# Layer 0's bias: channels sorted by sign, sums of two groups of keys folded into one last product

## The chip, the cores and the metric

The kernel runs on one core of a Trainium2 chip. The core has a matrix engine (TensorE, PE in the profile), a vector engine (VectorE, DVE), an activation engine (ScalarE, ACT), a general engine (GpSimd, POOL), and SyncE (SP), which here only issues DMAs. They share an on-chip memory of 128 partitions (SBUF) and the matrix engine's output memory (PSUM). The metric is the device time of one execution in microseconds (us); the median of several runs counts.

## What is computed

The program is four layers on an image tensor of shape (2, 512, 32, 32). Layer 0 is an attention whose keys are sampled at learned places, followed by an MLP; layers 1 to 3 are other attentions and aren't touched. Layer 0 has 2 x 8 heads, 1024 queries and 64 keys per head. Each pair of query and key gets a bias from a small network with 128 hidden channels:

```python
pos = grid_q[:, :, None, :] - grid_kv[:, None, :, :]
bias = jnp.sign(pos) * jnp.log1p(jnp.abs(pos))
bias = jax.nn.relu(bias @ cpb_w1 + cpb_b1)
bias = jax.nn.relu(bias @ cpb_w2 + cpb_b2)
bias = (bias @ cpb_w3 + cpb_b3).reshape(b, GROUPS, H * W, Hd * Wd)
sim = jnp.einsum('bhid,bhjd->bhij', qh, kh) + bias
attn = jax.nn.softmax(sim, axis=-1)
```

The second product, 128 x 128 channels for 16 x 1024 x 64 pairs, is the bulk of the layer's work. The change concerns what happens between it and the third product, `@ cpb_w3`, which sums 128 channels, each with its weight, to one number.

## The kernel before

**The weights.** `last_weights` and `fold_weights` (L252 to L280) prepare the third product. The magnitude of each `cpb_w3` is multiplied into the columns of `cpb_w2` and into the bias, which a Relu lets through, so that only its sign is left. The 128 hidden channels are cut into four blocks q of 32 channels; row r of each block has its own sign. `flip` holds the sign of blocks 0 to 2 relative to block 3, `ends` that of block 3.

**The quads.** The work goes in quads of four keys, 256 in all: for each head u (16), each o (8) and each jj (2). A quad (u, o, jj) makes these steps:

- `first_hidden` (L633): DVE writes the first hidden layer of the four keys, four tiles of 128 channels x 1024 queries, one custom add with Relu each, for the quad that comes next. The two parts of the sum come from `table`, which loads the positions (L572, a DMA on SyncE with two buffers) and scales them on GpSimd (L574) and DVE (L618).
- `second_hidden` (L664): for each block q, eight products of 128 rows and 32 columns give a PSUM tile whose 128 partitions are four keys x 32 channels. ScalarE applies Relu with bias (L669) into a tile `h2q` of SBUF; there are 2, 3, 2 and 5 buffers for the four q.
- The four blocks are added into one tile with their signs: block 0 is flipped on ScalarE (L671), block 1 on GpSimd where jj is 1 (L673) and on ScalarE where it is 0 (L675), block 2 on GpSimd (L680). Block 0 goes into 1 by an accumulating DMA that GpSimd issues (L656), block 2 into 3 by an add on GpSimd (L682), and block 1 into 3 by another accumulating DMA, `join`, which is issued in the next quad after its own q = 1.
- `last_product` (L696): for each (u, o), four products of 128 rows and 32 columns (two jj, two halves of the queries) go to four column tiles of the array. The stationary operand is a window of `ends` with four columns that aren't zero, one for each key of the quad; over the eight o they fill 32 rows of the scores of the head.

```python
z = self.second_hidden(u, o, jj, h1, i + 1 == len(quads))
if jj == 1:
    held.append((u, o, (first, z)))
else:
    first = z
    if len(held) == 2:
        v, last, zs = held.pop(0)
        self.last_product(v, last, zs, sims, ps_s)
```

**The order.** In layer 0 the order of the instructions on PE, ACT, DVE and POOL is the order in which the program writes them down; each engine works through its own list and waits where an operand or a buffer isn't ready. SyncE's list is ordered by the framework's scheduler. Steps for the next pair of heads (`offsets`, `sampled`) and for the head that was finished (`attend`, `projection`) are put between the quads, one per quad. After the last quad come the last products of o = 6 and 7, the softmax of the last head and the output projection (`share`, L236; `project_one`, L795), in which DVE makes the final adds (L654, L682) itself.

**The start.** Until the first quad, about 21 us, `offsets` runs for the first pair of heads, with a convolution as products by diagonal matrices (L422, L425), and matmuls of ones (L152) fill TensorE. L597 spreads the first positions over all partitions; L561 turns x, and L480 makes the second q.

Of the kernel before, what the change touches and what calls it, by code (L numbers as in the profile page):

```python
# [34 lines left out]
    ("cpb_w1", 2), ("cpb_b1", 1), ("b2r", 4), ("w3r", 4), ("cpb_b3", 1),  # L35
# [11 lines left out]
NGRID = G_MID + 1  # L47

# [6 lines left out]
class Net:  # L55
# [40 lines left out]
    def layer0(self):  # L96
# [3 lines left out]
        with ExitStack() as ctx:  # L100
# [15 lines left out]
            self.weights = self.last_weights(keep)  # L116
# [22 lines left out]
            nc.vector.tensor_copy(self.taps, self.colr("dw_w", len(TAPS)))  # L139
            self.jj = 1  # L140
# [3 lines left out]
            with self.tc.manual_schedule(engines=engines):  # L144
# [9 lines left out]
                warm(11)  # L154
                for n, _ in enumerate(self.offsets(pairs[0], 0, ps)):
                    if n == 1:
                        warm(5)
                    elif n == 2:
                        first_tr = self.turn(pairs[0], 0, ps)
                        for t in (1, 2):  # L160
                            self.normed(pairs[t], t, nc.gpsimd)
                    elif n == 4:
                        warm(11)
# [5 lines left out]
                quads = [(u, o, jj) for u in range(2 * BP) for o in range(8) for jj in range(2)]  # L169
# [10 lines left out]
                held, self.join = [], None  # L180
                for i, (u, o, jj) in enumerate(quads):
                    self.jj = jj
                    if o == 1 and jj == 1 and u % 2 == 0 and u // 2 + 1 < BP:
# [7 lines left out]
                    z = self.second_hidden(u, o, jj, h1, i + 1 == len(quads))  # L191
                    if jj == 1:
                        held.append((u, o, (first, z)))
                    else:
                        first = z
# [18 lines left out]
                self.last_product(*held[0], sims, ps_s)  # L214
# [4 lines left out]
                self.last_product(*held[1], sims, ps_s)  # L219
# [29 lines left out]
    def last_weights(self, keep):  # L249
# [4 lines left out]
        nc = self.nc  # L254
        self.w3row = keep.tile([P, P], F32, tag="row", name="w3row")
        nc.scalar.dma_start(self.w3row, self.io["cpb_w3"].partition_broadcast(P))
        yield
        w3 = self.colr("w3r", 4)
        self.magb = keep.tile([P, 4], F32, tag="magb", name="magb")
        nc.vector.scalar_tensor_tensor(self.magb, w3, -1.0, w3, ALU.mult, ALU.max)  # L260
        nc.vector.tensor_tensor(self.magb, self.magb, self.colr("b2r", 4), ALU.mult)
        sign = keep.tile([P, 4], F32, tag="sign", name="sign")
        nc.vector.tensor_scalar(sign, w3, 0.0, 2.0, ALU.is_ge, ALU.mult)
        nc.vector.tensor_scalar(sign, sign, -1.0, None, ALU.add)
        self.flip = keep.tile([P, 3], F32, tag="flip", name="flip")
        nc.vector.tensor_tensor(self.flip, sign[:, 0:3], sign[:, 3:4].to_broadcast([P, 3]), ALU.mult)
        yield
        self.ends = keep.tile([P, 60], F32, tag="ends", name="ends")
        nc.gpsimd.memset(self.ends, 0.0)
        for k in range(4):  # L270
            rows = slice(32 * k, 32 * k + 32)
            nc.gpsimd.tensor_copy(self.ends[rows, 28 + k : 29 + k], sign[rows, 3:4])
        yield
        nc.vector.tensor_copy(self.ys, self.grid[:, G_Y : G_Y + NB])
        yield

    def fold_weights(self):
        nc, row = self.nc, self.w3row
        nc.vector.scalar_tensor_tensor(row, row, -1.0, row, ALU.mult, ALU.max)
        nc.vector.tensor_tensor(self.l0w2, self.l0w2, row, ALU.mult)  # L280
# [9 lines left out]
    def odd(self):  # L290

        while self.jj == 0:
            yield

    def advance(self, behind, enough):

        self.jj = 1
# [1664 lines left out]
```

## Time and profile before

| What | us |
|---|---|
| Median of 3 runs (lowest 3308.89, highest 3309.51) | 3309.51 |
| The profiled execution | 3310.24 |
| Its span, from first to last instruction | 3308.4 |
| First and last record of L664 (layer 0's second product) | 21.4 and 1975 |
| PE busy with L664 / L696 | 1790.1 / 133.3 |
| DVE busy with L633 | 1180.8 |
| ACT busy with L669 / L671 / L675 | 1121.7 / 291.3 / 145.6 |
| POOL busy with L682 / L656 / L680 / L673 | 610.5 / 451.6 / 446.5 / 143.6 |

The granted clock of TensorE was 1.00 throughout. In the lines of the profile, "L664" is line 664 of the kernel; "h<-hp,magb" says what is written from what, by tile names without numbers; "128x1024" is partitions x elements, "128*32" the size of the stationary operand; x16384 counts instructions. A product in fp32 shows as two records. A releaser behind "<-" is what ended the idle time before the instruction. "PEld" is the weight load. Records of TensorE overlap, so their mean duration isn't what one costs; the chain (the work that ended last, in order of time) and windows serve for that.

### The profile page before, as it was taken

The page shows a single profiled execution, that of the slowest core. Times are in us where ns is not written, and L with a number is a line of the kernel's source. Part 1 is how long each engine was busy: PE and PEld are TensorE (multiplying, and loading weights), DVE is VectorE, ACT ScalarE, POOL GpSimd, SP SyncE. Part 2 cuts the span into 40 slices and gives each one's busy share as a digit, 9 for nine tenths or more (in the row PEclk, how much of TensorE's full clock was granted, in tenths as well). Part 3 has the DMA queues.
Part 4 walks back from the last instruction along what each step waited for, and adds up shares of the span by engine and source line. Part 5 has one row for each costly group of instructions (what it writes and reads, how often), then busy time and mean ns, then how long its engine had stood idle before and what let it go on. Part 6 is the DMA issues. An engine that isn't in the chain of part 4 may idle for free.

```text
span 3308.4 us, 59878 instructions
## 1 busy us (share of the span) xinstructions
PE 3293.4 (100%) x24966; PEld 1223.5 (37%) x24966; DVE 2367.5 (72%) x2735; ACT 2038.2 (62%) x2139; POOL 2190.8 (66%) x1682
## 2 busy tenths in 40 slices
PE   9999999999999999999999999999999999999999
PEld 4332333332333333333333334444465533455333
DVE  7877777877776677777777665564565689855897
ACT  7887887888887588887887771111121366222662
POOL 6887887887877687887887874333223458634575
PEclk9999999999999999999999999999999999999999
DMA  7787887787787687887788762111000100000001
GB/s 181 160 163 152 161 165 154 160 164 154 162 158 142 119 162 150 162 162 155 159 159 180 160 133 112 39 51 38 0 1 0 39 1 1 14 1 13 1 1 52
DMA packets 102671, 342.64 MB, mean 104 GB/s; under 512 B 12656, under 2 KB 14832, under 8 KB 99312
## 3 DMA queue, kind: packets, MB, share of 16 engines
q0 software_dynamic: 73296, 266.90, 41.3%
q1 hardware_dynamic: 28080, 69.75, 7.5%
q8 instruction: 201, 3.29, 0.4%
q10 hardware_dynamic: 1008, 2.00, 0.2%
q14 instruction: 86, 0.70, 0.1%
HBM read 67.27 MB, written 4.46 MB: 22 GB/s over the span
## 4 chain that ended last, share of the span: by engine, by line
PE 91%; DVE 5%; POOL 2%; issue 1%; DMA 1%; ACT 0%; DVEq 0%; POOLq 0%; ACTq 0%
PE hp L664 50%; PE s L1512 5%; PE o L1541 5%; PE sim L696 3%; PE qk30P L1287 1%; PE qk20P L1287 1%; PE m_2P L842 1%; PE m_7P L842 1%; PE m_6P L842 1%; PE m_4P L842 1%; PE m_1P L842 1%; PE qk31P L1287 1%; PE qk21P L1287 1%; PE m_5P L842 1%; PE m_0P L842 1%; PE m_3P L842 1%
## 5 line engine op out<-in xcount | busy, mean ns | idle before, releaser
L664 PE MATMUL hp<-h,w 128*32 128x512 f32 x16384 | 1790.1, 592 | 1.0 <-ACT h L669 1.0
L633 DVE CUSTOM_DVE_ANT_1 h<-tx,bank 128x1024 f32<-128x1024 f32 (+1 forms) x1028 | 1180.8, 1210 | 362.2 <-PE hp L664 290.9
L669 ACT ACTIVATE h<-hp,magb 128x1024 f32<-128x1024 f32 x1024 | 1121.7, 1111 | 352.7 <-PE hp L664 342.0
L664 PEld LDWEIGHTS hp<-h,w 128*32 128x32 f32 x16384 | 528.1, 110 | 1212.0 <-issue 1158.0
L656 POOL DMA_DIRECT2D h<-h x509 | 451.6, 1021 | 356.3 <-ACT h L675 293.5
L682 POOL TENSOR_TENSOR h<-h,h 128x1024 f32<-128x1024 f32 x255 | 610.5, 2394 | 21.3
L680 POOL TENSOR_SCALAR h<-h,flip 128x1024 f32<-128x1024 f32 x256 | 446.5, 1744 | 1.0 <-ACT h L669 0.9
L1516 ACT ACTIVATE e<-s 128x1024 f32<-128x1024 f32 x256 | 262.0, 1025 | 181.2 <-PE s L1512 174.1
L671 ACT ACTIVATE h<-h,flip 128x1024 f32<-128x1024 f32 x256 | 291.3, 1138 | 0.0
L1541 PE MATMUL o<-e,v 64*64 64x512 f32 x2048 | 265.2, 589 | 2.5 <-DVE q L1580 2.5
L1512 PE MATMUL s<-q,k 64*64 64x512 f32 x2048 | 265.9, 591 | 0.0
L1523 POOL TENSOR_TENSOR some<-some,e 128x1024 f32<-128x1024 f32 x64 | 167.8, 2622 | 26.5 <-ACT e L1516 23.8
L1521 POOL TENSOR_TENSOR some<-e,e 128x1024 f32<-128x1024 f32 x32 | 76.1, 2378 | 141.7 <-DVE sum L1530 102.7
L673 POOL TENSOR_SCALAR h<-h,flip 128x1024 f32<-128x1024 f32 x128 | 143.6, 1122 | 30.2 <-ACT h L669 28.9
L675 ACT ACTIVATE h<-h,flip 128x1024 f32<-128x1024 f32 x128 | 145.6, 1138 | 0.0
L1528 DVE TENSOR_TENSOR sum<-sum,e 128x1024 f32<-128x1024 f32 x64 | 124.2, 1940 | 29.6 <-ACT e L1516 27.0
L696 PE MATMUL sim<-h,ends 128*32 128x512 f32 x1024 | 133.3, 592 | 0.0
L1541 PEld LDWEIGHTS o<-e,v 64*64 64x64 f32 x2048 | 77.9, 133 | 145.3 <-issue 134.9
L812 POOL TENSOR_TENSOR mlp_w<-mlp_w 128x512 f32<-128x512 f32 x16 | 21.8, 1360 | 159.5 <-DMA mlp_w<-in_mlp_w 121.4
L1512 PEld LDWEIGHTS s<-q,k 64*64 64x64 f32 x2048 | 76.5, 133 | 133.2 <-issue 117.2
L903 ACT ACTIVATE mh<-mh,cols 128x512 f32<-128x512 f32 x64 | 46.1, 721 | 124.3 <-DVE mh L921 65.4
L1526 DVE TENSOR_TENSOR sum<-e,e 128x1024 f32<-128x1024 f32 x32 | 81.1, 2534 | 31.7 <-ACT e L1516 31.7
(544 smaller groups left out, 3253.4 us busy)
## 6 DMA issues: line engine op xcount, KB each, us to landing
h<-h POOLq DMA_DIRECT2D x509, 512.0 KB, 6.4
lb<-logs SPq DMA_DIRECT2D x63, 512.0 KB, 5.4
mlp_w<-in_mlp_w SPq DMA_DIRECT2D x16, 1024.0 KB, 4.8
x<-in_x SPq DMA_DIRECT2D x8, 512.0 KB, 8.0
qkw<-in_l_qk SPq DMA_DIRECT2D x2, 2048.0 KB, 7.6
out<-x SPq DMA_DIRECT2D x15, 256.0 KB, 2.0
vw<-in_l_v SPq DMA_DIRECT2D x2, 1024.0 KB, 7.7
projw<-in_l_proj SPq DMA_DIRECT2D x2, 1024.0 KB, 4.7
```

Source lines behind the costliest of these rows:

```text
L633: self.nc.vector._custom_dve(TENSOR_ADD_SAT, out=h1[r][:, k, cut, :], in0=x[:, jj, 2 * r + k, :].unsqueeze(1).to_broadcast([P, H // parts, ...
L656: nc.gpsimd.dma_start(to, what, accum_op=ALU.add)
L664: nc.tensor.matmul(hp[rows, cut], lhsT=self.l0w2[:, 32 * q : 32 * q + 32], rhs=h1[k][:, cut], start=True, stop=True)
L669: nc.scalar.activation(y, hp, AF.Relu, bias=self.magb[:, q : q + 1])
L671: nc.scalar.activation(ys[0], ys[0], AF.Copy, scale=self.flip[:, 0:1])
L680: nc.gpsimd.tensor_scalar(y, y, self.flip[:, 2:3], 1.0, ALU.mult, ALU.mult)
L682: (nc.vector if final else nc.gpsimd).tensor_tensor(y, y, ys[2], ALU.add)
L696: nc.tensor.matmul(sims[u][at : at + 32, :], lhsT=self.ends[:, 28 - 4 * o : 60 - 4 * o], rhs=z[jj][:, h * HF : (h + 1) * HF], start=(o == ...
L842: self.nc.tensor.matmul(acc[p], lhsT=w[:, a, k, p * P : (p + 1) * P], rhs=right(r, k), start=k == 0, stop=k == 1)
L1512: nc.tensor.matmul(s[halves[c], par, :], lhsT=ks[p][rows, at : at + DH], rhs=qs[p][rows, cut], start=True, stop=True)
L1516: nc.scalar.activation(e, s, AF.Exp, scale=DH**-0.5)
L1541: nc.tensor.matmul(o[halves[par], r, :], lhsT=v[n // 2][rows, n % 2, at : at + DH], rhs=e[rows, par, :], start=(n == 0), stop=(n == NB - 1),)
```

## The change

Channels are no longer taken in the order of the weights. `sorted_weights` computes on the chip, from the signs of `cpb_w3`, a place for each channel: blocks 1, 2 and 3 get positive channels in their first rows and negative ones below, in groups of six (two neighbouring rows x three blocks), so that within such a group all signs are equal; what is left over goes to block 0. A permutation matrix, scaled by the magnitudes, is built by comparing each rank with a constant table `places` (a new input, 128 x 244); products with it sort the columns of `cpb_w2` (now laid out transposed) and the bias. So blocks 1 to 3 can be added without flips, and rows 2i and 2i + 1 of the sum have the same sign. Only block 0 is flipped, on ScalarE.

Quads are now (u, o, half): the same four keys belong to one jj = o % 2, and the two halves of an o are eight neighbouring keys. `join` is an add on GpSimd instead of a DMA. After the second half's join, three DMAs fold: in the first half's sum the odd rows are added to the even ones; in the second half's sum the even rows are added to the odd ones; both accumulate and are issued by GpSimd. Then SyncE copies the odd rows of the second half's sum into the first's. That tile now holds 16 rows for each of eight keys, and one last product serves two o's: four products (two jj, two halves of the queries) with a window of `folded` in which eight columns aren't zero. For the last o = 7 the halves aren't folded; `single_product` takes them one by one. The tile h23 gets 6 buffers instead of 5.

```diff
-                quads = [(u, o, jj) for u in range(2 * BP) for o in range(8) for jj in range(2)]
+                quads = [(u, o, half) for u in range(2 * BP) for o in range(8) for half in range(2)]
...
-                    z = self.second_hidden(u, o, jj, h1, i + 1 == len(quads))
-                    if jj == 1:
-                        held.append((u, o, (first, z)))
-                    else:
-                        first = z
+                    z = self.second_hidden(u, o, half, h1, i + 1 == len(quads))
+                    if half == 0:
+                        batch.append((o % 2, z))
+                    elif o % 2 == 1:
+                        held.append((u, o, batch))
+                        batch = []
                         if len(held) == 2:
                             v, last, zs = held.pop(0)
                             self.last_product(v, last, zs, sims, ps_s)
...
                 self.join(True)
                 self.advance(after, lambda: False)
-                self.last_product(*held[0], sims, ps_s)
+                (_, _, (ready, first)), = held
+                self.last_product(u, o, [ready], sims, ps_s)
+                self.single_product(u, o, 0, first[1], sims)
...
-                self.last_product(*held[1], sims, ps_s)
+                self.single_product(u, o, 1, z, sims)
...
+        pool.affine_select(
+            out=before, in_=self.all, compare_op=ALU.is_ge, fill=0.0, base=-1, pattern=[[1, P]], channel_multiplier=-1
+        )
...
+        vec.tensor_scalar(c["pos"], w3, 0.0, None, ALU.is_ge)
+        nc.tensor.matmul(at_bank[:, 0:1], lhsT=before, rhs=c["pos"], start=True, stop=True)
+        nc.tensor.matmul(at_bank[:, 1:2], lhsT=self.all, rhs=c["pos"], start=True, stop=True)
...
+        vec.tensor_scalar(perm, self.places[:, 0:P], c["rank"], c["mag"], ALU.is_equal, ALU.mult)
+        got = self.bank[:, 384:512]
+        nc.tensor.matmul(got, lhsT=self.l0w2, rhs=perm, start=True, stop=True)
+        small = self.counts.rearrange("p (q i) -> p q i", i=2)
+        for q in range(4):
+            for k in range(4):
+                rows = slice(32 * k, 32 * k + 32)
+                nc.tensor.matmul(
+                    small[rows, q, :], lhsT=perm[:, 32 * q : 32 * q + 32], rhs=two, start=True, stop=True
+                )
...
+        nc.scalar.copy(self.l0w2, got)
...
+        nc.scalar.copy(self.magb, small)
...
-            y = self.hid2.tile([P, N], F32, tag=f"h2{q}", bufs=(2, 3, 2, 5)[q], name=f"h2_{u}_{o}{jj}{q}")
+            y = self.hid2.tile([P, N], F32, tag=f"h2{q}", bufs=(2, 3, 2, 6)[q], name=f"h2_{u}_{o}{half}{q}")
             ys.append(y)
-            nc.scalar.activation(y, hp, AF.Relu, bias=self.magb[:, q : q + 1])
-            if q == 1:
-                nc.scalar.activation(ys[0], ys[0], AF.Copy, scale=self.flip[:, 0:1])
-                if jj == 1:
-                    nc.gpsimd.tensor_scalar(y, y, self.flip[:, 1:2], 1.0, ALU.mult, ALU.mult)
+            nc.scalar.activation(y, hp, AF.Relu, bias=self.magb[:, q, 0:1])
+            if q == 0:
+                nc.scalar.activation(y, y, AF.Copy, scale=self.flip)
+            elif q == 1:
+                if final:
+                    nc.vector.tensor_tensor(y, y, ys[0], ALU.add)
                 else:
-                    nc.scalar.activation(y, y, AF.Copy, scale=self.flip[:, 1:2])
-                add(y, ys[0])
+                    nc.gpsimd.dma_start(y, ys[0], accum_op=ALU.add)
                 if self.join:
                     self.join(final)
-            elif q == 2:
-                nc.gpsimd.tensor_scalar(y, y, self.flip[:, 2:3], 1.0, ALU.mult, ALU.mult)
             elif q == 3:
                 (nc.vector if final else nc.gpsimd).tensor_tensor(y, y, ys[2], ALU.add)
-        self.join = lambda final: add(ys[3], ys[1], final)
+
+        def join(final, z=ys[3], other=ys[1], first=self.first_z, fold=half == 1 and not final):
+            (nc.vector if final else nc.gpsimd).tensor_tensor(z, z, other, ALU.add)
+            if fold:
+                nc.gpsimd.dma_start(first[0::2, :], first[1::2, :], accum_op=ALU.add)
+                nc.gpsimd.dma_start(z[1::2, :], z[0::2, :], accum_op=ALU.add)
+                nc.sync.dma_start(first[1::2, :], z[1::2, :])
+
+        self.join, self.first_z = join, ys[3]
         return ys[3]
...
+        at = 24 - 4 * (o - o % 2)
         for h in range(2):
-            for jj in range(2):
-                at = h * NJ + jj * 32
-                nc.tensor.matmul(
-                    sims[u][at : at + 32, :],
-                    lhsT=self.ends[:, 28 - 4 * o : 60 - 4 * o],
-                    rhs=z[jj][:, h * HF : (h + 1) * HF],
-                    start=(o == 0),
+            for jj, z in zs:
+                self.nc.tensor.matmul(
+                    sim[h * NJ + jj * 32 : h * NJ + jj * 32 + 32, :],
+                    lhsT=self.folded[:, at : at + 32],
+                    rhs=z[:, h * HF : (h + 1) * HF],
+                    start=(o < 2),
                     stop=False,
                 )
+
+    def single_product(self, u, o, half, z, sims):
+        jj, at = o % 2, 28 - 4 * (o - o % 2) - 4 * half
+        for h in range(2):
+            self.nc.tensor.matmul(
+                sims[u][h * NJ + jj * 32 : h * NJ + jj * 32 + 32, :],
+                lhsT=self.single[:, at : at + 32],
+                rhs=z[:, h * HF : (h + 1) * HF],
+                start=False,
+                stop=False,
+            )
```

The rest of `sorted_weights` is a dozen and a half one-column operations on DVE and GpSimd that turn the two counts into ranks, and the scaling of `folded` and `single` by the row signs. They are spread over `offsets` of the first pair, as `last_weights` was; the normalisation of a third x tile moves from DVE to GpSimd.

## The prediction

> **What bounds the kernel now.** I read the page's busy table and its chain first: they say which engine ends the program, and which lines stand on that chain.
>
> ```profile
> PE 3293.4 (100%) x24966; PEld 1223.5 (37%) x24966; DVE 2367.5 (72%) x2735; ACT 2038.2 (62%) x2139; POOL 2190.8 (66%) x1682
> ...
> PE hp L664 50%; PE s L1512 5%; PE o L1541 5%; PE sim L696 3%; PE qk30P L1287 1%; PE qk20P L1287 1%; PE m_2P L842 1%; PE m_7P L842 1%; PE m_6P L842 1%; PE m_4P L842 1%; PE m_1P L842 1%; PE qk31P L1287 1%; PE qk21P L1287 1%; PE m_5P L842 1%; PE m_0P L842 1%; PE m_3P L842 1%
> ```
>
> Half of the chain is the hidden product (L664) and 3% the last product (L696), which the change halves. A share over the span doesn't say whether TensorE has gaps in layer 0, so next the windows by stage (busy us and count of each engine, granted clock, DMA share, GB/s):
>
> ```profile
> core 0: us, PE busy (x) PEld busy (x) DVE busy (x) ACT busy (x) POOL busy (x), PEclk, DMA share, GB/s
> ...
> 500.00:1000.00 500.00, 500.00 (x4712) 152.85 (x4708) 376.82 (x417) 411.40 (x411) 403.92 (x328) 1.00 0.79 159
> ```
>
> TensorE is never idle in the middle of layer 0, and ScalarE and GpSimd come next. So TensorE work taken out here shortens the program, as long as nothing else gets as slow. The chain in order of time gives its pieces (start, us):
>
> ```profile
> 90.45 0.86 PE sim L696 x8
> 91.31 13.73 PE hp L664 x128
> 105.04 0.86 PE sim L696 x8
> ```
>
> One quad (four keys) is 64 records, 6.87 us; each two quads carry one last product, 8 records, 0.86 us. The groups of the window 100 to 1850 us give the other engines' prices (count | busy, mean ns | idle before):
>
> ```profile
> L664 PE MATMUL hp<-h,w 128*32 128x512 f32 x14644 | 1599.6, 592 | 0.7 <-ACT h L669 0.7
> ...
> L682 POOL TENSOR_TENSOR h<-h,h 128x1024 f32<-128x1024 f32 x229 | 548.2, 2394 | 19.1
> ...
> L673 POOL TENSOR_SCALAR h<-h,flip 128x1024 f32<-128x1024 f32 x114 | 127.9, 1122 | 28.1 <-ACT h L669 27.1
> ...
> L574 POOL TENSOR_SCALAR tx<-lb,cols 128x512 f32<-128x512 f32 x57 | 43.6, 764 | 0.0
> ```
>
> 14644 / 64 = 228.8 quads in 1750 us: 7.65 us a quad, 15.30 for two, of which 14.59 is the plain pattern above and the rest TensorE's side work. The mean of 592 ns isn't a price, since records overlap. For GpSimd's L680 the mean misleads too, which the timeline shows (start, us):
>
> ```profile
> 614.82 1.78 POOL L656 DMA_DIRECT2D h<-h  x2 [1.62 <-ACT h L675]
> 615.99 1.77 POOL L680 TENSOR_SCALAR h<-h,flip 128x1024 f32<-128x1024 f32 x1
> 617.84 2.39 POOL L682 TENSOR_TENSOR h<-h,h 128x1024 f32<-128x1024 f32 x1
> ```
>
> L680 begins while the DMA issues run (to 616.60) and ends at 617.76: it costs 1.16 us, not 1.74. The view of L656 gives an issue's price (ns min/median/max) and its landing:
>
> ```profile
> L656 POOL DMA_DIRECT2D h<-h x509: 852/882/1509, 29.8 to 1968.3; - x170
> ...
> DMA to landing us min/median/max: 4.4/6.4/13.1
> ```
>
> [...] L696's four 32-column products, two records each, fill 0.86 us together. [...]
>
> **The change, part by part.**
> *TensorE, removed.* Before: 16 u x 8 o = 128 last products of 0.86 = 110.1 us. After: one for two groups of o, the same four column tiles in the same order: 63 x 0.86 = 54.2. The last pair is taken apart: its folded part has two calls, its two single products two each; the first two lie on different tiles, so I take two rounds, 1.7 us (1.3 to 2.6). Gain 110.1 - 55.9 = **54.2 us** (53.3 to 54.6), all on the path.
>
> *GpSimd, for two quads.* Before: 4 issues x 0.88 + 2 x 2.39 (L682) + 2 x 1.16 (L680) + 1.12 (L673) + half a tx, 0.38 = 12.1 us. After the scalings are gone, the join of q1 into q3, a DMA before, is an add on GpSimd, and two fold DMAs come per two quads: (2 + 2) x 0.88 + 4 x 2.39 + 0.38 = 13.5 us, with some eight gaps of 0.07 about 14.0. TensorE needs 13.73 + 0.43 = 14.16 in the plain pattern and 15.30 - 0.43 = 14.87 on average. So GpSimd fits, barely, and what it falls behind in plain stretches it gets back at side work. No trace shows a fold DMA of 64 rows: half the rows could cost 0.45 us, or as much as the slowest issue seen, 1.51; I take 0.88, as for 128 rows.
>
> *ScalarE* loses L675 (1.14 us a second quad); q0's flip now goes ahead of q1's Relu, which ends at about 5.3 us into a quad (Relu at 2.0, flip, Relu: 3 x 1.1). In the same table it stands idle for 314 us before L669 alone. DVE's four custom adds stay.
>
> *The fold's waits.* Take the start of the next pair's first quad as zero. The q1 DMA goes out at 5.3, the join add runs to 8.6, the two fold issues to 10.4; from 9.5 the second lands after 4.4 to 6.4, at 14 to 16; SyncE's copy, 256 KB, takes between 2.0 (out<-x, as large) and 5.4 (lb<-logs): 16 to 21. TensorE asks for it after its fourth quad, at 27.5: 6 us to spare. Only a fold at the maximum of 13.1 would be 0.5 late. The copies stand on SyncE among the lb loads; an lb load placed ahead of a copy waits for DVE's reading of an older lb, done at about 7, so the copy isn't held, and an lb is needed two quads later by GpSimd's tx. The join add waits for the previous quad's q1 DMA, landed 1.4 us before at the median; queued behind it are the folds and the q3 add, for which ScalarE's next Relu waits only two quads later. The six h23 buffers give a half-1 sum back three quads after it is written. Bytes on GpSimd's queue fall from 509 x 512 KB to 255 x 512 + 254 x 256, so landings shouldn't get longer.
>
> *The start.* The sort adds one 128-column product (0.25 us, as one of L152's eleven in 2.72) and 16 products of two columns, two records each (32 x 0.07, from L360's four in 0.28): 2.4 us on TensorE between L597 and L561. DVE's dozen small operations (0.16 each) replace seven of before or fall in its wait for q; GpSimd takes over one xn while it has nothing else. But ScalarE sets when the second quad begins: before, it runs Relu, Relu, two flips and two Relus with waits from 24.5 to 31.5. Now its copies of the second q end at 26.4 instead of 23.9, and Relu, flip and three Relus without waits (5 x 1.12) end at 32.0. I take +0.6 us (0 to 2.5).
>
> *The end.* The last folded sum has only one quad to land:
>
> ```profile
> 1981.44 1.07 PE L696 MATMUL sim<-h,ends 128*32 128x512 f32 x8
> ...
> 1984.83 0.71 DVE L727 STREAM_TRANSPOSE t<-sim 128x512 f32<-128x512 f32 x1
> ```
>
> TensorE ends the last quad 13.7 us after zero, adds a round, and then waits for the copy until 16 to 21: 2 to 6 us. L236's first twelve records and the last single product stand behind that and move as much, but L727 behind them began only 1.5 us after the scores were complete (1983.4, at the end of L711), since DVE was busy. I take +3 us (0.5 to 5).
>
> *Sum.* -54.2 + 0.6 + 3 = -50.6. The profiled execution took 3310.24 us (span 3308.4); the median of the runs is 3309.51, 0.7 lower. 3309.5 - 50.6 = **3259 us**; the ends of the terms give 3255 to 3264.
>
> **The rivals.**
> *GpSimd paces part of layer 0 (0.14).* For it: 14.0 against 14.16 us. Against it: two quads of buffers. Were a fold issue at 1.51 us, two quads would take 14.0 + 2 x 0.63 = 15.3, 0.4 over TensorE's 14.87: 128 x 0.4 = 51 us, nothing gained. Halfway, at 1.2 us, it is 14.65: over in the plain stretches only (0.5 in perhaps half of the 128), 30 us lost: 3289.
> *Slower: GpSimd becomes the bound (0.06).* The same queue, if all four issues pay: from 0.88 + (15.3 - 14.0) / 4 = 1.2 us each it takes more than now. At 1.51 each: 14.0 + 4 x 0.63 = 16.5 us, 128 x (16.5 - 14.87) = +209 on the forecast: 3468. Against it: the median issue is 0.88, and an add stays within 2.34 and 2.42 us in all 255 cases of before.
> *The folded sums come late (0.05).* Each us beyond the 6 spare costs 63 us; two landings of 8.5 instead of 6 and 5 are just hidden, so it takes several queues together. With 0.5 us late on each: 3259 + 31 = 3290.
> *It doesn't do what it says:* were the product no longer four wide, nothing would be gained; the order over the column tiles is that of before, so I leave it no chance of its own.
>
> **How the numbers follow.** The forecast has 0.75, pacing 0.14, late sums 0.05, the bound 0.06. A measurement can tell about 0.2%, 6.6 us, from no change. Pacing ends within that in about 0.03 and on the slower side in 0.01; so faster 0.90, same 0.03, slower 0.07. For 8 in 10 the range takes the forecast's 3255 to 3264, some us below for an end that hides wholly, and the cheaper half of pacing: 3251 to 3280.
>
> **What would show it.** Right: about 516 records of the last product instead of 1024; pieces of 27.5 us of hidden product between 0.86 us rounds in the chain; TensorE without idle time in layer 0; GpSimd at over 90% there with adds of 2.39 us; layer 0 some 50 us shorter, later layers equal. Wrong: TensorE waiting for ScalarE, and ScalarE for GpSimd or a DMA, in every pair of quads; fold issues over 1.2 us; waits of the last product for a copy; a start or an end longer by more than 5 us.

## The result, and the profile after

The changed kernel takes 3260.2 us (median of 4 runs, 3259.2 to 3260.6) against 3309.5 (3308.9 to 3310.8) for the kernel before: a ratio of 0.985, 95% interval 0.9833 to 0.9867. The profiled execution's span fell from 3308.4 to 3258.3 us, by 50.1. The new line numbers: hidden product L704, Relu L709, flip L711, last product L742 (taken singly L753), q1's accumulating DMA L716, adds on GpSimd L720 (block 2 into 3) and L723 (join), fold L725 and L726, SyncE's copy L727, tx L622.

The page's busy table of the kernel after, and its chain by engine:

```profile
PE 3243.6 (100%) x24496; PEld 1210.7 (37%) x24496; DVE 2388.4 (73%) x2742; ACT 1949.1 (60%) x2013; POOL 2348.2 (72%) x1557
...
PE 81%; POOL 11%; DVE 5%; issue 2%; ACT 0%; DMA 0%; DVEq 0%; POOLq 0%; ACTq 0%; SPq 0%
```

TensorE has 470 records less (508 and 8 of last products instead of 1024, and some new ones at the start) and GpSimd is 157 us busier. Before, nearly all of layer 0 in the chain was TensorE; now GpSimd has 11%. In the chain in order of time, GpSimd's adds appear from 1512 us on. That doesn't mean that TensorE waited for them. The windows by stage of the kernel after (busy us and count of TensorE, its weight load, VectorE, ScalarE and GpSimd, then clock, DMA share, GB/s) tell whether it did:

```profile
60.00:500.00 440.00, 440.00 (x4164) 134.56 (x4160) 345.66 (x371) 351.79 (x342) 405.96 (x265) 1.00 0.70 147
500.00:1000.00 500.00, 500.00 (x4692) 152.40 (x4688) 399.91 (x437) 400.03 (x389) 458.32 (x302) 1.00 0.69 146
1000.00:1500.00 500.00, 499.59 (x4456) 155.99 (x4450) 377.69 (x407) 375.96 (x366) 427.67 (x283) 1.00 0.65 135
1500.00:1900.00 400.00, 400.00 (x3752) 121.61 (x3748) 306.68 (x334) 318.29 (x305) 370.16 (x240) 1.00 0.69 146
```

From 1500 on TensorE is busy for 400.00 of 400 us. The chain is followed backward, and the way back from the last folded sum goes through GpSimd's queue; with two engines nearly level it can stay there. GpSimd is at 92% in the middle (404 of 500 us before, 458 after). One window isn't full: 1000 to 1500 lacks 0.41 us. That small number is the visible end of a larger loss, the 3.8 us of the table below: records of TensorE overlap (L704's last 0.59 us each at the median, while 256 of them fill 27.47 us, 0.11 each), so they cover most of its short waits.

The chain of the kernel after shows the new rhythm: a last product every four quads, where there was one every two.

```profile
111.53 0.86 PE sim L742 x8
112.39 27.47 PE hp L704 x256
139.85 0.86 PE sim L742 x8
```

To see where the 50.1 us are, I counted in both traces, for each line of TensorE, the time from the start of one record to the start of the next:

| Stretch | before, us | after, us | difference |
|---|---|---|---|
| to the second quad's start | 31.51 | 32.84 | +1.3 |
| from there to the last hidden product: last products | 110.19 | 54.23 | -56.0 |
| the same: hidden products | 1757.1 | 1760.9 | +3.8 |
| the same: all other lines, each | | | within 0.02 |
| from there to layer 0's MLP (first m_0P) | | | +0.7 |
| MLP and layers 1 to 3 | 1300.3 | 1300.4 | 0.1 |

The +3.8 is in the main one place. A quad takes 6.87 us at the median, in both kernels. After, those that begin at 1265.4, 1272.8 and 1283.0 us take 7.4, 9.4 and 7.8, together 3.9 more than the same three before; the small differences elsewhere cancel. The timeline of the kernel after around the first of them (start, us; GpSimd and VectorE):

```profile
1265.11 3.52 POOL L723 TENSOR_TENSOR h<-h,h 128x1024 f32<-128x1024 f32 x1
...
1265.99 5.53 DVE L509 TENSOR_SCALAR xn<-x,bn1s,cols 128x1024 f32<-128x1024 f32 x1
1267.46 3.50 POOL L720 TENSOR_TENSOR h<-h,h 128x1024 f32<-128x1024 f32 x1
...
1271.44 4.60 DVE L680 CUSTOM_DVE_ANT_1 h<-tx,bank 128x1024 f32<-128x1024 f32 x4
```

VectorE's normed pair (xn) begins while GpSimd's join add runs, and ends only after the second add, which followed without a gap. The first hidden layer of the next quad (L680) stands behind it, and TensorE behind that. The views of the normed pair's line before and after (ns min/median/max):

```profile
L461 DVE TENSOR_SCALAR xn<-x,bn1s,cols x8: 803/805/814, 5.0 to 1531.4; 128x1024 f32<-128x1024 f32 x8
```

```profile
L509 DVE TENSOR_SCALAR xn<-x,bn1s,cols x7: 814/1831/5532, 4.9 to 1486.3; 128x1024 f32<-128x1024 f32 x7
```

The operation that took 0.81 us in the kernel before took 5.53 here, over two adds in a row, and ended 0.56 us after the second. That GpSimd's adds are what held it is so far my reading of this one stretch; the runs below test it.

My theory was thus: the gain is 64 rounds on TensorE and nothing else, the added work on GpSimd and in the DMAs is hidden, and some 5 us are lost again, most of them to VectorE held by GpSimd's adds. The rivals: relief of ScalarE and GpSimd pays part of the gain; the fold costs TensorE time; the loss at 1272 us has another cause; GpSimd already sets the pace. All times below are medians beside runs of the kernel before on the same chip, which had medians of 3309.0 to 3309.4.

### The profile page after: what moved, and what is told of

Its sections match the earlier page's. It is cut to its first block, busy times and chain, and to the rows that moved or that the text cites. A ratio compares the mean times of both kernels' runs of the same rounds, so it can differ in the third digit from the quotient of the medians.

```text
span 3258.3 us, 59109 instructions
## 1 busy us (share of the span) xinstructions
PE 3243.6 (100%) x24496; PEld 1210.7 (37%) x24496; DVE 2388.4 (73%) x2742; ACT 1949.1 (60%) x2013; POOL 2348.2 (72%) x1557
## 4 chain that ended last, share of the span: by engine, by line
PE 81%; POOL 11%; DVE 5%; issue 2%; ACT 0%; DMA 0%; DVEq 0%; POOLq 0%; ACTq 0%; SPq 0%
PE hp L704 41%; PE s L1569 5%; PE o L1598 5%; POOL h L723 5%; POOL h L720 4%; PE qk30P L1344 1%; PE qk20P L1344 1%; PE m_7P L899 1%; PE m_6P L899 1%; PE m_4P L899 1%; PE m_2P L899 1%; PE m_0P L899 1%; PE qk31P L1344 1%; PE qk21P L1344 1%; PE m_5P L899 1%
## 5 line engine op out<-in xcount | busy, mean ns | idle before, releaser
L704 PE MATMUL hp<-h,w2s 128*32 128x512 f32 x16384 | 1784.0, 592 | 0.5 <-DVE h L680 0.2
L680 DVE CUSTOM_DVE_ANT_1 h<-tx,bank 128x1024 f32<-128x1024 f32 (+1 forms) x1028 | 1180.3, 1210 | 301.9 <-PE hp L704 240.3
L709 ACT ACTIVATE h<-hp,magb 128x1024 f32<-128x1024 f32 x1024 | 1133.1, 1110 | 378.8 <-PE hp L704 368.2
L704 PEld LDWEIGHTS hp<-h,w2s 128*32 128x32 f32 x16384 | 530.6, 110 | 1212.5 <-issue 1184.6
L720 POOL TENSOR_TENSOR h<-h,h 128x1024 f32<-128x1024 f32 x255 | 819.1, 3212 | 1.6 <-ACT h L709 1.6
L723 POOL TENSOR_TENSOR h<-h,h 128x1024 f32<-128x1024 f32 x254 | 751.3, 2958 | 0.0
L716 POOL DMA_DIRECT2D h<-h x255 | 303.0, 1188 | 192.3 <-ACT h L709 179.6
L711 ACT ACTIVATE h<-h,flip 128x1024 f32<-128x1024 f32 x256 | 294.3, 1150 | 8.4
L726 POOL DMA_DIRECT2D h<-h x127 | 175.4, 1381 | 1.0 <-issue 1.0
L725 POOL DMA_DIRECT2D h<-h x127 | 149.0, 1173 | 0.0
L1332 POOL TENSOR_TENSOR sq<-q 128x512 f32<-128x512 f32 x32 | 33.2, 1041 | 96.1 <-DVE q L1351 54.2
```

The lines of the kernel that those rows point to most:

```text
L680: self.nc.vector._custom_dve(TENSOR_ADD_SAT, out=h1[r][:, k, cut, :], in0=x[:, 4 * half + 2 * r + k, :].unsqueeze(1).to_broadcast([P, H // ...
L704: nc.tensor.matmul(hp[rows, cut], lhsT=self.l0w2[:, 32 * q : 32 * q + 32], rhs=h1[k][:, cut], start=True, stop=True)
L709: nc.scalar.activation(y, hp, AF.Relu, bias=self.magb[:, q, 0:1])
L711: nc.scalar.activation(y, y, AF.Copy, scale=self.flip)
L716: nc.gpsimd.dma_start(y, ys[0], accum_op=ALU.add)
L720: (nc.vector if final else nc.gpsimd).tensor_tensor(y, y, ys[2], ALU.add)
```

## The experiments

**Sorted, but not folded.**

```diff
-                nc.gpsimd.dma_start(first[0::2, :], first[1::2, :], accum_op=ALU.add)
-                nc.gpsimd.dma_start(z[1::2, :], z[0::2, :], accum_op=ALU.add)
-                nc.sync.dma_start(first[1::2, :], z[1::2, :])
...
-                            self.last_product(v, last, zs, sims, ps_s)
+                        v, last, zs = held[0][0], held[2][1], (held[0], held[2]) if half == 0 else (held[1], held[3])
+                        for hh in range(2):
+                            self.single_product(v, zs, hh, sims, ps_s)
```

> The channels stay sorted, the flips stay gone and the join add stays on GpSimd, but nothing is folded: every quad's 32-row sums go through the single product, 128 rounds in layer 0 as before instead of 64, and the two accumulating DMAs and SyncE's copy are left out. Theory (the gain is 64 TensorE rounds of 0.87 us, and nothing else pays): 3260.2 + 64 x 0.87 = 3316, or about 3312 if the 3.8 us stall of VectorE's normed pair goes with the lighter GpSimd; in any case slower than the kernel before by 0.05 to 0.25%. Rival (part of the gain comes from relief of ScalarE and GpSimd, since flips and a join DMA are gone too): clearly under 3309.5, 3260 if all of it does.

Measured: 3322.4 us (3321.1 to 3323.6), ratio 1.0039, interval 1.0024 to 1.0054. So the rival falls: with the flips and the join DMA gone, but all last products there, nothing is gained. It is 6 us more than the theory's 3316, and 0.39% over the kernel before, above the theory's 0.25%. The quads explain that: added up, they take 6.6 us more than in the changed kernel, in short stalls at regular places, where VectorE's small operations were held (its log operation of 128x64, 0.22 us at best, took 5.15 at the median). Nor do these stalls hide a gain: against the run without stalls below (the join add as a DMA) the quads take 10.3 us more, and without them this kernel would be at about 3312, an estimate, still not under 3309.5. The rest of the difference to the changed kernel, (3322.4 - 3260.2 - 6.6) / 64 = 0.87 us, is one round.

**The fold left out.**

```diff
-            if fold:
-                nc.gpsimd.dma_start(first[0::2, :], first[1::2, :], accum_op=ALU.add)
-                nc.gpsimd.dma_start(z[1::2, :], z[0::2, :], accum_op=ALU.add)
-                nc.sync.dma_start(first[1::2, :], z[1::2, :])
```

> The two accumulating DMAs of the fold and SyncE's copy are left out, all else is the changed kernel; the product for two quads reads unfolded sums, so half of the sums is left out of the result. Theory (the fold lies wholly beside TensorE): 3260.2 less at most the 1.2 us that the last folded product waited and, if the lighter GpSimd no longer holds VectorE, 3.8: 3255 to 3260. Rival (GpSimd's issues or the fold's landing cost TensorE time all along layer 0): under 3245, 1 us or so for each of the 128 pairs of quads would be 128 us.

Measured: 3273.8 us (3273.7 to 3275.6), ratio 0.9891, interval 0.9876 to 0.9906. Both expectations fail: with less work the kernel is 13.6 us slower than with the fold. The timeline of this run at one of its long quads (start, us):

```profile
417.92 5.20 DVE L441 TENSOR_TENSOR log<-log,pos 128x64 f32<-128x64 f32 x1
418.03 2.67 POOL L723 TENSOR_TENSOR h<-h,h 128x1024 f32<-128x1024 f32 x1
...
420.36 2.66 POOL L720 TENSOR_TENSOR h<-h,h 128x1024 f32<-128x1024 f32 x1
```

An operation on 64 elements a partition takes 5.20 us and ends 0.1 us after GpSimd's second add. In the changed kernel the fold's two issues stand between the two adds in every second quad. The difference shows best in an operation of 128x2 that begins just ahead of a join add in both kernels; its view in the changed kernel and in this run (ns min/median/max):

```profile
L417 DVE TENSOR_SCALAR at<-at x8: 168/1609/3061, 14.8 to 1596.8; 128x2 f32<-128x2 f32 x8
```

```profile
L417 DVE TENSOR_SCALAR at<-at x8: 169/2793/5391, 15.9 to 1609.5; 128x2 f32<-128x2 f32 x8
```

In the changed kernel the four long ones begin at a join add that the fold's issue follows, and end with that add, after 3.05 us; here the four long ones take 5.39 and end with the second add. (The log operation met only the end of a q3 add in the changed kernel: 0.76 to 1.38 us.) Here the adds are always in a row, and the quads lose 19.5 us in all, at the same places of five of the eight pairs of heads and beside one normed pair, instead of 3.7 once. What these are to be compared with comes from the next run.

**The join add as a DMA again, without the fold.**

```diff
-            (nc.vector if final else nc.gpsimd).tensor_tensor(z, z, other, ALU.add)
+            if final:
+                nc.vector.tensor_tensor(z, z, other, ALU.add)
+            else:
+                nc.gpsimd.dma_start(z, other, accum_op=ALU.add)
```

> Like the run without the fold (the fold's three DMAs are left out, so half of the sums is missing from the result), and the join add of every quad is an accumulating DMA again, as in the kernel before, instead of GpSimd's tensor_tensor: GpSimd then has one add a quad and never two in a row. Theory (the run without the fold took 3273.8 because GpSimd's two adds, 2.4 us each and one straight after the other, held VectorE's small operations for up to 5.4 us some 20 times): without adds in a row these operations take 0.2 to 0.9 us again, no quad but the first is over 7.3 us, and the time is 3273.8 - 19.8 = 3254. Rival (VectorE is held by something that the sorted layout or the missing fold brought): stays at 3270 or more.

Measured: 3254.6 us (3254.4 to 3255.1), ratio 0.9835, interval 0.982 to 0.985; the theory's number to within 1 us. The same line of VectorE without the fold, first with the join add on GpSimd, then with the DMA:

```profile
L441 DVE TENSOR_TENSOR log<-log,pos x7: 220/5199/5218, 159.7 to 1633.3; 128x64 f32<-128x64 f32 x7
```

```profile
L441 DVE TENSOR_TENSOR log<-log,pos x7: 215/217/220, 159.6 to 1615.2; 128x64 f32<-128x64 f32 x7
```

The two kernels differ in this one add. So the join add on GpSimd, with the q3 add straight behind it, costs the 19 us, and neither the sorted layout nor the missing fold does.

**The normed pairs on ScalarE.**

```diff
-        (ahead or nc.vector).tensor_scalar(
-            xn, self.xs[b][t], self.s1[:, t : t + 1], self.col("bn1_b", t), ALU.mult, ALU.add
-        )
+        if b == 0:
+            (ahead or nc.vector).tensor_scalar(
+                xn, self.xs[b][t], self.s1[:, t : t + 1], self.col("bn1_b", t), ALU.mult, ALU.add
+            )
+        else:
+            nc.scalar.activation(
+                xn, self.xs[b][t], AF.Identity, scale=self.s1[:, t : t + 1], bias=self.col("bn1_b", t)
+            )
```

> The second image's four normed pairs go from VectorE to ScalarE (an activation with the same scale and bias); the first image's stay. Theory (the one 3.8 us stall of TensorE at 1272 us is VectorE's normed pair held for 5.5 us by GpSimd's adds): every quad of layer 0 is then within 6.8 to 7.6 us and the time is 3260.2 - 3.8 = 3256.4. Rival (the stall comes from something else at that place, such as the transfer of the pair or the sampling work): the quad stays long, and the time stays within 1 us of 3260.2. Second rival (ScalarE, now with 1.2 us more at that place, holds TensorE instead): 3258 to 3261 with a wait on ScalarE at about 1272 us.

Measured: 3256.2 us (3255.7 to 3256.8), ratio 0.9839, interval 0.9826 to 0.9852. The runs don't overlap with those of the changed kernel, which is 4 us slower. No quad but the first is over 7.16 us, and the quads add up to 1765.9, as in the kernel before (1765.7) and in the run above (1765.9). So the loss was the held normed pair. This version beats both kernels. Against the run above, which has no fold and the join as a DMA (3254.6), 1.6 us are left for all that the fold and the join add on GpSimd cost; in the changed kernel the last folded product alone waits for 1.2.

**The third early pair back on VectorE.**

```diff
-                        for t in (1, 2, 3):
+                        for t in (1, 2):
                             self.normed(pairs[t], t, nc.gpsimd)
...
+            if o == 0:
+                self.normed(pairs[3], 3, nc.vector)
             next(self.weights)
             x = tables["x"][:, jj, :, :]
```

> The third of the three normed pairs that GpSimd makes ahead at the start goes back to VectorE, to the place where the kernel before had it (behind the masked logs of the first table). Theory (GpSimd's third pair, 1.2 us, held VectorE's log operation for 1.02 us instead of 0.23, and this is 0.8 of the 1.3 us that the start became longer): second quad starts at about 32.0 us instead of 32.84, time 3259.4. Rival (the start is paced by the sort itself, or by the pair on VectorE when it is there): the second quad starts at 32.8 or later, time 3260.2 to 3261.

Measured: 3259.7 us (3259.2 to 3260.0), ratio 0.9849, interval 0.9835 to 0.9862; the second quad begins at 32.39 us. That looks like half of what the theory said, but it can't be told from chance: in the ten profiled executions that sort and have the pair on GpSimd, the second quad begins at 32.3 to 33.3 us, and the log operation that took 1.02 us in the changed kernel's took 0.22 to 0.28 in the other nine.

**Both edits.**

> The second image's normed pairs on ScalarE and the third early pair of the first image on VectorE, together. Theory (two independent losses, 3.9 us at 1272 us and 0.5 at the start): 3260.2 - 3.9 - 0.5 = 3255.8, faster than the changed kernel by 0.13% and than the kernel before by 1.6%. Rival (one of them moves where GpSimd's adds meet VectorE's operations, and a stall comes back): 3259 or more.

Measured: 3256.2 us (3255.7 to 3256.4), ratio 0.9839, interval 0.9826 to 0.9853, against 3256.2 with the ScalarE edit alone. The second quad begins at 32.81. The edit at the start is worth nothing that shows; what makes the start longer stays open.

**More work for GpSimd.** How near GpSimd is to setting the pace can't be read from 92%. Four runs load it. The first two have the changed kernel with one multiplication by one more for two quads, on half of the sums or on all:

```diff
             (nc.vector if final else nc.gpsimd).tensor_tensor(z, z, other, ALU.add)
+            if more:
+                nc.gpsimd.tensor_scalar(z[:, 0:512], z[:, 0:512], 1.0, 1.0, ALU.mult, ALU.mult)
```

> GpSimd gets one operation more for two quads: it multiplies half of the first quad's sums (128x512) by one in place after the join add, before the fold. About 0.75 us by the tx operation of the same size. Theory (GpSimd has about 14.0 us of work for two quads, TensorE 14.16 without and 14.87 with the other work of layer 0): 14.7 is still under TensorE's mean, so the time stays within 0.2% of 3260, up to 10 us more where GpSimd falls behind for a few pairs. Rival (GpSimd has no room left at all): 127 x 0.75 = +95, 3355. Second rival (GpSimd has much more room than that, because its instructions overlap): 3260.

> The same operation on the whole sums, 128x1024, about 1.12 us by the kernel before's flip of that size. Theory (GpSimd 15.1 us for two quads against TensorE's mean of 14.87): GpSimd paces layer 0, and the time grows by about 127 x 0.25 = 32, to about 3290 (3275 to 3310). Rival (no room left at all): 127 x 1.12 = +142, 3402. Second rival (much room): 3260.

Measured: half, 3257.7 us (3256.7 to 3257.9), ratio 0.9844, interval 0.9829 to 0.986; all, 3268.6 (3266.0 to 3268.9), ratio 0.9875, interval 0.9859 to 0.989. The half one makes the kernel 2.5 us *faster*: the adds meet VectorE's operations elsewhere, the normed pair takes 3.19 us at most, and the longest of the later quads 7.8. The whole one costs 8, and lies under the theory's 3275 to 3310; where the 8 us are is told with the next two runs. To keep the held pair out of it, the next two have the normed pairs on ScalarE, with one and two multiplications:

```diff
+            if more:
+                nc.gpsimd.tensor_scalar(z, z, 1.0, 1.0, ALU.mult, ALU.mult)
+                nc.gpsimd.tensor_scalar(z, z, 1.0, 1.0, ALU.mult, ALU.mult)
```

> The second image's normed pairs on ScalarE (so that GpSimd's adds can't hold them), and one multiplication by one of the first quad's whole sums on GpSimd for two quads, 1.04 us each. In the changed kernel GpSimd is busy for 458.3 of 500 us in the middle of layer 0, 13.4 of 14.6 us for two quads. Theory (so there are 1.2 us of room for two quads): 14.4 still fits; 3256 to 3262. Rival (the 8 us that this multiplication cost before came from GpSimd pacing, not from its adds meeting VectorE): 3264 or more.

> The same with two such multiplications, 2.08 us for two quads. Theory: 13.4 + 2.08 = 15.5 us on GpSimd against 14.6, so GpSimd paces layer 0 and the time grows by 127 x 0.87 = 110, to about 3366 (3340 to 3390); TensorE then waits for GpSimd's sums, GpSimd is over 98% busy. Rival (GpSimd's instructions overlap, so the room is larger): under 3300.

Measured: one, 3265.9 us (3265.6 to 3267.5), ratio 0.9868, interval 0.9852 to 0.9885; two, 3383.6 (3383.4 to 3385.2), ratio 1.0226, interval 1.0209 to 1.0243. The window of the run with two:

```profile
500.00:1000.00 500.00, 474.99 (x4384) 138.88 (x4380) 372.40 (x403) 364.48 (x364) 493.20 (x345) 1.00 0.65 135
```

Now TensorE has gaps, and GpSimd paces. The 3383.6 lie in the theory's 3340 to 3390. Of one multiplication the theory said 3256 to 3262 and the rival 3264 or more; the rival is right on the number. But only part of it is in layer 0's middle: of the 11.8 us between the profiled executions, 6 are in quads of 7.1 to 7.8 and 5 at the end. There TensorE waits 3.4 us for the last folded sum instead of 1.5, and then runs slower. The same twelve records in the chain of the ScalarE edit and of this run:

```profile
1923.89 5.35 PE ob L246 x12
```

```profile
1933.57 7.46 PE ob L246 x12
```

From 1931 to 1942 us the granted clock of this run is 0.69 (0.999 over its whole span); at the end of layer 0 of the changed kernel, and of the ScalarE edit, it is 1.00. The run with a whole multiplication on the changed kernel waits 3.8 us at the same place, and its clock over the span is 0.999 as well: of its 8 us some 3.6 are in the quads. That the wait lowered the clock is not shown. Whether the long quads wait for GpSimd itself or for VectorE's still held small operations (3.07 us at the median for one of 128x64) isn't told apart. The timeline of the run with two shows what the operations cost in place (start, us):

```profile
618.01 1.74 POOL L721 DMA_DIRECT2D h<-h  x1
619.00 3.17 POOL L728 TENSOR_TENSOR h<-h,h 128x1024 f32<-128x1024 f32 x1
622.26 1.04 POOL L730 TENSOR_SCALAR h<-h 128x1024 f32<-128x1024 f32 x1
623.39 1.04 POOL L731 TENSOR_SCALAR h<-h 128x1024 f32<-128x1024 f32 x1
624.40 2.38 POOL L725 TENSOR_TENSOR h<-h,h 128x1024 f32<-128x1024 f32 x1
626.74 0.88 POOL L721 DMA_DIRECT2D h<-h  x1
627.37 2.68 POOL L728 TENSOR_TENSOR h<-h,h 128x1024 f32<-128x1024 f32 x1
629.70 1.17 POOL L733 DMA_DIRECT2D h<-h  x1
630.35 1.40 POOL L734 DMA_DIRECT2D h<-h  x1
630.93 3.25 POOL L725 TENSOR_TENSOR h<-h,h 128x1024 f32<-128x1024 f32 x1
```

Durations mislead here, since a record begins while the issue before it still runs (the join add at 619.00, the issue before it up to 618.01 + 1.74 = 619.75). Starts tell: from an issue to the next instruction 0.58 to 0.65 us, where nothing else is waited for, from an add to the next 2.33. From the join add (619.00) to the q3 add (624.40) it is 5.40 us, so the two multiplications cost 5.40 - 2.33 = 3.1, not 2.08: the first begins at 622.26, 0.09 us after the end of the add whose result it reads. Two quads take 15.6 us here (32 pairs in 500 us), so without the extra 3.1 GpSimd needs at most 12.5 us, and has about 2.1 to spare of TensorE's 14.6 (34.2 pairs in 500 us of the changed kernel). These are estimates from the starts and the windows. One multiplication, with the wait that it brings, takes nearly all of that: 5.40 - 1.04 - 2.33 = 2.0.

**The join as a DMA, with the fold.** The edit is that of the run without fold above, on the changed kernel.

> The changed kernel with its fold, but the join add of every quad is an accumulating DMA again, as in the kernel before. The fold's first DMA reads what the join's DMA writes, so GpSimd waits for its landing (4 to 5 us after the issue) with the next quad's add and issues queued behind it. Theory (GpSimd's order is what matters): for two quads two adds 4.8, four issues 2.5 to 3.5, the fold's two issues 1.3 to 2.4, the tx operation 0.75 and the wait 4 to 5 make 13.4 to 16.5 against 14.6; the middle, 15, gives 127 x 0.4 = +50, about 3306 (3255 to 3500), with GpSimd's wait for a DMA ahead of the fold's issue in the trace. Rival (the waits fall into GpSimd's idle time): 3255, since no two adds are in a row.

Measured: 3715.7 us (3714.7 to 3716.1), ratio 1.1227, interval 1.1208 to 1.1246. The mechanism is the theory's, the size isn't (it said about 3306, at most 3500). The waits of GpSimd in this run (us in all, times, longest; L726 issues the join, L728 and L729 the fold):

```profile
POOL h L729 <- DMA h<-h: 579.3, 123, 7.6
POOL h L728 <- DMA h<-h: 280.4, 124, 4.8
...
POOL h L726 <- DMA h<-h: 100.1, 69, 3.7
```

I had counted one wait; there are two, one for each half's join, 2.3 and 4.7 us on average, and a third ahead of the join itself in 69 of its 255 issues. GpSimd isn't even busy (284 of 500 us): it stands, with the next quad's add and issues behind it. Through them ScalarE waits for its buffers (its L709 for the DMA 528.4 us in all) and TensorE for ScalarE (the hidden products 282.3 us, their weight loads 567.1). TensorE's granted clock was 0.972 over this run's span (0.95 to 0.96 in the windows of layer 0), not 1.00, which is in the time too: at most 3714 x 0.028 = 104 us, an estimate, of the 455 over the changed kernel. So the join add on GpSimd, 2.4 us a quad, is what lets the fold go out without a wait.

This run also shows that GpSimd's adds needn't be in a row to hold VectorE for long (start, us):

```profile
477.64 2.69 POOL L720 TENSOR_TENSOR h<-h,h 128x1024 f32<-128x1024 f32 x1
...
478.46 6.81 DVE L416 SCALAR_TENSOR_TENSOR at<-at,grid 128x2 f32<-128x2 f32 x1
...
480.01 1.06 POOL L622 TENSOR_SCALAR tx<-lb,cols 128x512 f32<-128x512 f32 x1
...
480.74 1.19 POOL L716 DMA_DIRECT2D h<-h  x1
...
481.34 1.50 POOL L726 DMA_DIRECT2D h<-h  x1
...
481.90 3.34 POOL L720 TENSOR_TENSOR h<-h,h 128x1024 f32<-128x1024 f32 x1
```

The operation of 128x2 stays held over an add, the tx operation, two issues and a second add, for 6.81 us, and ends with that one (0.03 us after it). What decides whether it gets through between two of GpSimd's instructions stays open.

## Why the prediction was right, step by step

- *The bound.* TensorE had no idle time in the middle, and taking its work out shortened the program by just that work. The unfolded run confirms it from the other side.
- *The removal* (-54.2): measured -56.0 up to the last hidden product, 64 rounds of 0.87 us (126 before, 62 after). The rounds at the very end, which the prediction counted here, are in the end's figure. The prediction took two rounds, 1.7 us, for the folded and the two single products. The folded and the first single product ran side by side, as it assumed, 1.05 us together, and the last single product took about 1.0, so 2.0 in all, within its 1.3 to 2.6. The chain of the kernel after shows it (start and us; two DMAs, the fold and the copy, and then the products; L753's first records add only 0.01 us each):

```profile
1919.71 4.33 DMA h<-h
...
1924.12 2.23 DMA h<-h
...
1926.49 0.62 PE sim L742 x2
1927.11 0.01 PE sim L753 x2
1927.13 0.41 PE sim L742 x2
1927.54 0.01 PE sim L753 x2
...
1932.90 0.55 PE sim L753 x2
...
1933.48 0.41 PE sim L753 x2
```

- *GpSimd's 14.0 us for two quads*: mis-sized. The issue was priced at 0.88 us by its record; from start to start it is 0.6, and two quads take at most about 12.5. The bounds of 0.45 and 1.51 for a fold issue were needless: by their records the fold's issues take 1.16 and 1.38, and by their starts 0.64 and 0.58. The conclusion (it fits beside TensorE) held, with more room than said.
- *The fold's waits* (6 us to spare): right. The fold's DMAs land in 4.4 and 5.3 us at the median, and no folded product in the middle waited for a copy. The DMA share fell from 0.79 to 0.69.
- *The start* (+0.6, 0 to 2.5): +1.3 in the profiled executions; by the spread above, 0.8 to 1.8 over the one execution of before. The sort's 16 small products took 0.36 us in the chain, not the 2.2 that they were priced at. With its one large product (0.22) and three operations on VectorE (0.52) the sort holds 1.1 us of the chain up to the first quad; that this is what the start lost isn't shown.
- *The end* (+3, 0.5 to 5): +0.7. The folded sum was waited for, but for 1.16 us instead of 2 to 6. The last copy came 2.23 us after its issue and the fold 4.33, the quick ends of what was allowed for.
- *Not foreseen* (+3.8): VectorE held by GpSimd's adds. The prediction put four adds for two quads on GpSimd, counted their time there, and didn't ask which engine they would hold. The kernel before already showed holds: its log operation took about 1 us at the median, and in five of seven cases it began with GpSimd's scaling of block 1 (L673) and ended 0.07 us after it:

```profile
L393 DVE TENSOR_TENSOR log<-log,pos x7: 967/1064/1705, 161.5 to 1673.8; 128x64 f32<-128x64 f32 x7
```

Against the prediction's terms the removal gave 1.8 more, the start cost 0.7 more, the end 2.3 less and the stall 3.8: these sum to 0.4, so that 3259 lay so near to 3260 is partly luck. The bound and the way of the gain were right without it.

The rivals: pacing by GpSimd and late sums didn't come. Of the slower one the mechanism is real, since the run with two more multiplications ends 2.3% above the kernel before. But its point lies about 2 us of GpSimd's time further on, not at issues of 1.2 us.

## What to carry to other kernels

Work moved to an engine that has time wasn't free here, since beside that engine's adds another was held (0.81 us became 5.53, and the join add on GpSimd cost 19 us where no fold stood between the adds): look for short operations on VectorE whose maximum is many times their minimum, and for what GpSimd was doing at that moment. What GpSimd's instructions cost is read from the distance of their starts in a stretch without gaps, and the room it has by loading it until the time moves. When the fold's DMAs read what a DMA had just written, GpSimd's queue stood still for the landing (2.3 and 4.7 us on average), with all that was behind it, and the kernel took 3715.7 us instead of 3260.2.

## What the runs showed of the hardware

- A VectorE operation on 64 elements a partition, 0.22 us alone, took 5.2 us beside two GpSimd adds of 128x1024 in a row. One on 2 elements took 5.39 there, and 3.05 where a DMA issue followed the first add; with a tx operation and two issues between the adds such an operation was held for 6.81 us. VectorE's custom adds of 128x1024 (L633 before, L680 after), with one operand in PSUM, took 1.20 to 1.23 us throughout, in the kernels before and after.
- A hold needn't lengthen a quad: with the normed pairs on ScalarE, operations of 128x2 and 128x64 still take up to 3.1 us, and no quad but the first is over 7.16.
- Less work can be slower (the fold left out, +13.6 us) and more work faster (half a multiplication added, -2.5), since it moves the moment at which the two engines meet.
- On GpSimd, a multiplication that reads the result of the add before it started 3.26 us after that add's start (619.00 to 622.26), where the next independent instruction started after 2.33 (627.37 to 629.70).
- After TensorE had waited 3.4 and 3.8 us at the end of layer 0 (one more multiplication on GpSimd), the granted clock over the span was 0.999; in the run with the wait of 3.4 it was 0.69 from 1931 to 1942 us, and twelve records took 7.46 us instead of 5.35. In the changed kernel, with a wait of 1.2 us, it was 1.00 there. Whether the wait is the cause no run tests.
